# Cross-attention and FFN on one core: weighted sums in four column parts of 32, with their denominators in the second PSUM bank of the same tile

## The chip, the cores and the metric

The kernel runs on one core of a Trainium2 chip. Its engines work side by side, each in the order of its own queue: TensorE (PE, with its weight loads shown as PEld), VectorE (DVE), ScalarE (ACT), GpSimd (POOL) and SyncE (SP), which issues most transfers. The metric is the device time of one execution in microseconds (us), as the median of several runs.

## The reference

One sequence of 2048 rows of width 256 attends to 1601 context rows of width 192 plus one learned "null" key, with 16 heads of 64, and then passes through a three-layer network with weights of +1 and −1:

```python
x = layer_norm(_layernorm(x), g_norm)         # 2048 x 256
q = x @ Wq;  k, v = split(context @ Wkv)      # 16 heads of 64
k, v = [null_k; k], [null_v; v]               # 1602 keys
sim = einsum('bhid,bhjd->bhij', q * s, k * s) # s * s = 1/8
attn = softmax(where(mask, sim, -max))
out = einsum('bhij,bhjd->bhid', attn, v)
x = x0 + layer_norm(out @ Wout, g_out)
x = x + ffn(_layernorm(x))                    # 512 -> 1024 -> 1024 -> 256, relu * 2
```

All inputs but the masks are float32.

## The kernel before

The attention works in 32 units. A unit is a pair of heads (p, 8 of them) by a block of 512 query rows (b, 4 of them); in the code `u` counts the units. Keys are taken in KC = 13 chunks of 128 (the last has 66). The scores stand transposed, keys on the partitions and queries along the free axis, so that the exponentials can be used as the moving operand of the weighted sums without another transpose.

From the second unit on, a unit runs as follows, and the order is written out by hand (`manual_schedule`), engine by engine:

1. For each key chunk k: the scores of both heads (TensorE, L391; the first two chunks add the negated maximum of each query, L415), then the exponential on ScalarE (L417, `e`). Between them TensorE computes one chunk of row maxima for the *next* unit (L361, L345) into a PSUM tile, and VectorE reduces it (L364, L348). GpSimd adds up the exponentials of all chunks into `acc` (L665, L667), one sum for each key partition.
2. VectorE combines the maxima of the next unit (L369).
3. The denominators of the *previous* unit. In 28 units ("quarters": all but units 0, 1, 30 and 31) `denominators` (L443) multiplies `acc` by a matrix of ones: four matmuls of 32 columns and 256 queries, two for each head, which lie side by side in one PSUM bank, on 128 partitions by 256 columns. VectorE then takes the reciprocal (L455), ScalarE spreads it over the head's rows with eight small copies (L461), and VectorE multiplies the previous unit's weighted sums by it (L462, `aoT`). Units 1, 30 and 31 do it in `divided` after the third weighted chunk instead (L468, L470); the last unit's own division comes later, within the network.
4. The weighted sums of this unit (`weighted`, L424): for each of the 13 chunks, two matmuls of 64 columns, one a head. Head 0 goes to partitions 0 to 63 and head 1 to partitions 64 to 127 of one bank of `av`. Each float32 matmul appears in the trace as two records, one for each of two passes.
5. ScalarE copies the sums out (L721). TensorE turns the maxima of the next unit (L374), multiplies the previous unit's `aoT` by the output weights (L432), projects queries (L213) and a part of the next pair's keys (L243, L248) or values (L303, L315).

PSUM is divided between two pools of two tiles each, each tile two banks wide ([128, 2, 512] float32): `flex` (maxima, denominators, the turned maxima, projections) and `spare` (the two score tiles, `av`, the output projection). In `spare` the order within a unit is sT_1, sT_0, av, po, so that `av` takes over the buffer of the odd chunks' scores. A tile that is asked for waits until the tile two places back in its pool has been read. The waits between engines are semaphores that the framework sets from what each instruction reads and writes.

After the attention come the residual and the network, in blocks of 512 rows as well.

## Time and profile before

Three runs took 1289.89, 1290.35 and 1291.47 us; the median is 1290.35. One execution was profiled:

| what | value |
|---|---|
| span of the profiled execution | 1288.7 us |
| TensorE busy | 1275.8 us (99%) |
| GpSimd busy | 1001.7 us (78%) |
| VectorE busy | 787.9 us (61%) |
| ScalarE busy | 717.7 us (56%) |
| granted TensorE clock, mean | 1.000 |
| scores (L391), TensorE | 448.5 us |
| weighted sums (L424), TensorE | 364.7 us |
| maxima (L361), TensorE | 276.8 us |
| denominators (L443), TensorE | 17.9 us |
| reciprocals of the denominators (L455), VectorE | 48.9 us |

Busy time is the time in which at least one instruction of the group was under way. Matmuls overlap, so that the sum of their durations is larger than the busy time, and a busy TensorE is not one at its peak. In a timeline a row gives the start in us, the duration, the engine, the line, the operation and the tiles (out<-in), the number of instructions that were merged, and in brackets the engine's idle time ahead and what ended it.

### The profile page before, as it was taken

The page shows a single profiled execution, that of the slowest core. Times are in us where ns is not written, and L with a number is a line of the kernel's source. Part 1 is how long each engine was busy: PE and PEld are TensorE (multiplying, and loading weights), DVE is VectorE, ACT ScalarE, POOL GpSimd, SP SyncE. Part 2 cuts the span into 40 slices and gives each one's busy share as a digit, 9 for nine tenths or more (in the row PEclk, how much of TensorE's full clock was granted, in tenths as well). Part 3 has the DMA queues.
Part 4 walks back from the last instruction along what each step waited for, and adds up shares of the span by engine and source line. Part 5 has one row for each costly group of instructions (what it writes and reads, how often), then busy time and mean ns, then how long its engine had stood idle before and what let it go on. Part 6 is the DMA issues. An engine that isn't in the chain of part 4 may idle for free.

```text
span 1288.7 us, 16385 instructions
## 1 busy us (share of the span) xinstructions
PE 1275.8 (99%) x6672; PEld 648.9 (50%) x6672; DVE 787.9 (61%) x817; ACT 717.7 (56%) x965; POOL 1001.7 (78%) x508
## 2 busy tenths in 40 slices
PE   8999999999999999999999999999999999999998
PEld 6334444444444444444444444444444443788887
DVE  7887866655665566556666666666666784644432
ACT  4766556655555555555565666666655667422120
POOL 5798988998889888989899889988998999801100
PEclk9999999999999999999999999999999999999999
DMA  5000000000000000000000000000000010000000
GB/s 145 22 1 5 1 1 13 5 1 1 13 5 2 1 13 5 1 1 13 5 1 1 1 14 5 1 1 5 1 17 1 1 41 1 1 9 9 17 17 17
DMA packets 16156, 13.19 MB, mean 10 GB/s; under 512 B 2688, under 2 KB 15552, under 8 KB 16080
## 3 DMA queue, kind: packets, MB, share of 16 engines
q1 hardware_dynamic: 14944, 11.02, 3.1%
q8 instruction: 52, 0.85, 0.3%
q10 hardware_dynamic: 656, 0.79, 0.2%
q0 software_dynamic: 480, 0.34, 0.2%
q14 instruction: 24, 0.20, 0.1%
HBM read 10.04 MB, written 2.10 MB: 9 GB/s over the span
## 4 chain that ended last, share of the span: by engine, by line
PE 96%; DVE 2%; DMA 1%; ACT 1%; issue 0%; SPq 0%; DVEq 0%; ACTq 0%
PE sT L391 29%; PE av L424 27%; PE ps L775 11%; PE max L361 7%; PE po L432 4%; PE psq L213 4%; PE ps L806 2%; PE psv L303 2%; PE psk L243 1%; PE sT L415 1%; PE den L443 1%; PE psv L315 1%; DMA x_sb<-in_x 1%; PE psk L248 1%; PE max L345 1%; ACT e L417 1%
## 5 line engine op out<-in xcount | busy, mean ns | idle before, releaser
L667 POOL TENSOR_TENSOR acc<-acc,e 128x1024 f32<-128x1024 f32 (+1 forms) x352 | 847.3, 2407 | 27.6
L364 DVE TENSOR_REDUCE mx<-max 128x2 f32<-128x1024 f32 x384 | 450.3, 1220 | 80.3 <-PE max L361 78.4
L417 ACT ACTIVATE e<-sT,maskb 128x1024 f32<-128x1024 f32 (+1 forms) x416 | 460.4, 1113 | 40.4 <-PE sT L391 9.1
L391 PE MATMUL sT<-qT,kT 64*128 64x512 f32 (+1 forms) x1664 | 448.5, 613 | 1.5 <-ACT e L417 0.9
L424 PE MATMUL av<-e,v 128*64 128x512 f32 (+1 forms) x1664 | 364.7, 594 | 0.2 <-ACT e L417 0.2
L361 PE MATMUL max<-kr,qr 64*128 64x512 f32 x768 | 276.8, 712 | 1.9 <-DVE mx L364 1.9
L424 PEld LDWEIGHTS av<-e,v 128*64 128x64 f32 (+1 forms) x1664 | 116.7, 137 | 233.5 <-issue 230.5
L391 PEld LDWEIGHTS sT<-qT,kT 64*128 64x128 f32 (+1 forms) x1664 | 128.2, 181 | 146.6 <-ACT e L417 133.3
L461 ACT COPY aoT<-r 32x256 f32<-32x256 f32 x224 | 90.1, 402 | 63.9 <-DVE r L455 61.6
L361 PEld LDWEIGHTS max<-kr,qr 64*128 64x128 f32 x768 | 75.3, 187 | 95.8 <-DVE mx L364 67.4
L665 POOL TENSOR_TENSOR acc<-e,e 128x1024 f32<-128x1024 f32 x32 | 75.6, 2361 | 61.4 <-ACT seen L655 52.2
L721 ACT COPY avs<-av 128x512 f32<-128x512 f32 x32 | 18.7, 585 | 159.7 <-PE av L424 159.7
L462 DVE TENSOR_TENSOR aoT<-avs,aoT 128x512 f32<-128x512 f32 x28 | 43.1, 1539 | 94.3 <-ACT aoT L461 94.3
L376 DVE TENSOR_TENSOR mT<-mt,pick 128x512 fp32r<-128x512 f32 x32 | 22.1, 689 | 106.9 <-PE mt L374 106.9
L775 PE MATMUL ps<-h0hi,w 128*128 128x512 f32 x256 | 79.5, 392 | 0.0
L775 PE MATMUL ps<-h0lo,w 128*128 128x512 f32 x256 | 78.9, 389 | 0.0
L122 POOL TENSOR_TENSOR y_sb<-y_sb,gout_sb 128x256 f32<-128x256 f32 x12 | 9.3, 775 | 86.7 <-DVE y_sb L89 86.7
L214 ACT ACTIVATE qr<-psq 128x512 fp32r<-128x512 f32 x32 | 19.1, 597 | 97.8 <-PE psq L213 95.1
L763 ACT ACTIVATE h1hi<-ps 128x1024 fp32r<-128x1024 f32 x16 | 16.4, 1026 | 98.9 <-PE ps L775 98.9
L764 DVE SCALAR_TENSOR_TENSOR h1lo<-ps,h1hi 128x1024 fp32r<-128x1024 f32 x16 | 19.6, 1223 | 67.8 <-ACT h1hi L763 67.8
L432 PE MATMUL po<-wo,aoT 128*128 128x256 f32 x256 | 60.6, 379 | 0.0
L213 PE MATMUL psq<-xnT,wq 128*128 128x512 f32 x124 | 58.4, 593 | 0.6 <-ACT xnT L498 0.6
(164 smaller groups left out, 1135.4 us busy)
## 6 DMA issues: line engine op xcount, KB each, us to landing
out_x<-o SPq DMA_DIRECT2D x7, 256.0 KB, 2.2
x_sb<-in_x SPq DMA_DIRECT2D x3, 512.0 KB, 8.2
wa<-in_wkv SPq DMA_DIRECT2D x8, 128.0 KB, 2.7
wq<-in_wq SPq DMA_DIRECT2D x8, 128.0 KB, 2.2
wo<-in_wout SPq DMA_DIRECT2D x8, 128.0 KB, 2.0
xnT<-in_k SPq DMA_DIRECT2D x1, 1024.0 KB, 5.7
wb<-in_wkv SPq DMA_DIRECT2D x15, 64.0 KB, 2.4
ctx_a<-in_ctxT SPq DMA_DIRECT2D x2, 256.0 KB, 8.1
```

The lines of the kernel that those rows point to most:

```text
L213: nc.tensor.matmul(ps[:, 0, :], weights[p][0][:, c, :], xnT[:, b, c, :], start=c == 0, stop=c == 1)
L361: nc.tensor.matmul(ps[:, j, :w], qr[rows, ts(t, 128)], kr[rows, ds(start, w)], start=True, stop=True)
L364: nc.vector.tensor_reduce(maxima[p, b][:, t, :, c], ps[:, :, :w], AX.X, ALU.max)
L391: nc.tensor.matmul(ps[:n, j, :], kT[rows, ds(128 * k, n)], qT[rows, :], start=k < 2, stop=k >= 2, skip_group_check=k >= 2,)
L417: nc.scalar.activation(e[:n], ps[:n], AF.Exp, bias=maskb[:n, k : k + 1])
L424: nc.tensor.matmul(av[ts(j, DH), 0, :], v[:n, k, ts(j, DH)], e[:n, j, :], start=k == 0, stop=k == KC - 1)
L432: nc.tensor.matmul(pv[:, t, :], aoT[:, ts(t, 128)], weights[p][3], start=True, stop=True)
L461: nc.scalar.copy(aoT[ds(64 * j + 32 * rows, 32), ts(h, 256)], r[ds(64 * j + 32 * h, 32), :])
L462: nc.vector.tensor_tensor(aoT, avs, aoT, ALU.mult)
L665: nc.gpsimd.tensor_tensor(acc, es[0], es[1], ALU.add)
L667: nc.gpsimd.tensor_tensor(acc[:m], acc[:m], es[k][:m], ALU.add)
L775: nc.tensor.matmul(ps[:, f, :], w(c)[:, ts(2 * g + f, 128)], parts[part][:, c, :], start=i == 0, stop=i == len(steps) - 1,)
```

## The change

The weighted sums of a chunk are issued as four matmuls of 32 columns in place of two of 64: each head is divided in halves of its width, and the four parts go to partitions 0, 32, 64 and 96 on, each at its own column position of the array. Both halves of a head stream the same exponentials `e[:n, i // 2, :]`.

The `av` tile is asked for before the denominators, and in the 28 "quarters" units the denominators go to the first 256 columns of its second bank, which was idle. The weighted sums still go to its first bank. The flex tile for denominators is gone in these units; units 1, 30 and 31 keep theirs. The lines below L424 move down by five.

```diff
         def weighted(p, k, e, av):
             v = pairs[p][1]
             n = rows_of(k)
-            for j in range(2):
+            for i in range(4):
                 nc.tensor.matmul(
-                    av[ts(j, DH), 0, :], v[:n, k, ts(j, DH)], e[:n, j, :], start=k == 0, stop=k == KC - 1
+                    av[ts(i, 32), 0, :],
+                    v[:n, k, ts(i, 32)],
+                    e[:n, i // 2, :],
+                    start=k == 0,
+                    stop=k == KC - 1,
+                    tile_position=(0, 32 * i),
                 )
...
                 quarters = last is not None and u not in (1, len(units) - 2, len(units) - 1)
+                av = spare(f"av_{p}_{b}")
                 if quarters:
-                    den = flex(f"den_{p}_{b}")[:, 0, :256]
+                    den = av[:, 1, :256]
                     denominators(last[3], den)
                     aoT = divided_quarters(*last[:3], den)
-                av = spare(f"av_{p}_{b}")
                 for k in range(KC):
                     weighted(p, k, es[k], av)
```

## The prediction

> **What bounds the kernel now.** I read the page first (busy shares, the chain that ended last), then the timeline around one denominator, then the waits of TensorE and VectorE there, then the order and the waits of the built programs. The page:

> ```profile
> span 1288.7 us, 16385 instructions
> PE 1275.8 (99%) x6672; PEld 648.9 (50%) x6672; DVE 787.9 (61%) x817; ACT 717.7 (56%) x965; POOL 1001.7 (78%) x508
> ...
> PE 96%; DVE 2%; DMA 1%; ACT 1%; issue 0%; SPq 0%; DVEq 0%; ACTq 0%
> ...
> L424 PE MATMUL av<-e,v 128*64 128x512 f32 (+1 forms) x1664 | 364.7, 594 | 0.2 <-ACT e L417 0.2
> ```

> TensorE (PE) is on the chain for 96% of the span: whatever stops its queue is paid in full, and time that another engine gains is worth nothing. The weighted sums (L424) are 27% of that chain.

> The stretch that the change edits lies between the scores and the weighted sums of a unit. There is one such stretch in each of 28 units. The timeline, one of them (start, duration, engine, line):

> ```profile
> 388.33 7.23 POOL L667 TENSOR_TENSOR acc<-acc,e 128x1024 f32<-128x1024 f32 x3
> 389.65 0.80 PE L361 MATMUL max<-kr,qr 64*128 64x512 f32 x2
> 390.33 1.11 ACT L417 ACTIVATE e<-sT,maskb 66x1024 f32<-66x1024 f32 x1 [0.20 <-PE sT L391]
> 390.38 0.16 PEld L443 LDWEIGHTS den<-acc,ones 128*32 128x32 f32 x8 [0.56 <-issue]
> 390.38 0.64 PE L443 MATMUL den<-acc,ones 128*32 128x256 f32 x8
> 390.50 1.23 DVE L364 TENSOR_REDUCE mx<-max 128x2 f32<-128x1024 f32 x1 [0.41 <-PE max L361]
> 390.95 0.20 PEld L424 LDWEIGHTS av<-e,v 128*64 128x64 f32 x4 [0.41 <-issue]
> 390.95 4.08 PE L424 MATMUL av<-e,v 128*64 128x512 f32 x18
> 391.43 0.14 PEld L424 LDWEIGHTS av<-e,v 128*64 128x64 f32 x2 [0.29 <-issue]
> 391.75 0.19 DVE L369 TENSOR_REDUCE mcol<-mx 128x8 f32<-128x32 f32 x1
> 391.86 1.75 DVE L455 RECIPROCAL r<-den 128x256 f32<-128x256 f32 x1
> 391.86 0.14 PEld L424 LDWEIGHTS av<-e,v 128*64 128x64 f32 x2 [0.29 <-issue]
> 392.29 0.14 PEld L424 LDWEIGHTS av<-e,v 128*64 128x64 f32 x2 [0.29 <-issue]
> ...
> 393.64 1.23 ACT L461 COPY aoT<-r 32x256 f32<-32x256 f32 x3 [2.20 <-DVE r L455]
> ```

> Two things are to be seen. TensorE goes from the denominators (390.38) to the weighted sums (390.95) at once. And VectorE is far behind it: it still has the last maximum (1.23), the combined maximum (0.19) and only then the reciprocal of the denominators, which ends at 391.86 + 1.75 = 393.61. Today nobody on TensorE waits for that: the reciprocal's reader is ScalarE, and its result is wanted only at the output projection after the weighted sums (402.4).

> **The change, part by part.**

> *The denominators in the second bank of av (28 units).* This removes a flex tile and adds a wait. In the built program of before, the first weighted matmul waits only for ScalarE's exponentials (L417). In that of the changed kernel, in all 28 units, it waits for VectorE's count to reach the reciprocal of the denominators in the same tile: the tile is guarded as if the two banks were one. The weighted sums overwrite no column that the reciprocal reads, but the semaphore holds them all the same. Behind that matmul in the in-order TensorE queue are all weighted sums, the transposed maxima (L374), the output projection, the next queries and keys or values, and so the next unit's scores; ACT, DVE and POOL wait for those.

> Price: the first weighted load starts at 390.95 and could start when the reciprocal is done, 393.61: 2.66 us here, 2.65 to 2.66 in all 28 units (mean 2.653). Add the step from VectorE's end to TensorE's start, which the profile shows where TensorE does wait for VectorE:

> ```profile
> 36.53 0.69 DVE L376 TENSOR_TENSOR mT<-mt,pick 128x512 fp32r<-128x512 f32 x1 [0.92 <-PE mt L374]
> 37.28 0.19 PEld L415 LDWEIGHTS sT<-mT,ones_r 64*128 64x128 f32 x2 [0.62 <-DVE mT L376]
> ```

> 37.28 − 37.22 = 0.06. So 2.71 a unit, 28 × 2.71 = 75.9 us, none of it beside other TensorE work, as nothing may overtake in that queue. The reciprocal can't come sooner: the maximum ahead of it waits for the last max matmul (390.45), and the denominators end (391.02) before VectorE is free, so their start doesn't matter.

> [...]

> *What the freed flex tile gives.* The denominators waited for the maximum two chunks back (L348), now for the exponential of k = 11; both are over by 390.3. The flex tiles that follow (mt, queries, keys or values, first maxima) are still two tiles behind an engine that is done, so no wait goes: 0. Spare tiles go round in the same order as before. The orders of ACT, DVE, POOL and SP are unchanged, and no DMA moves.

> *Four parts of 32 columns.* 104 instead of 52 weighted matmul records a unit, and as many weight loads. With two parts of 64 the loads come in pairs every 0.43 us (391.43, 391.86, 392.29): both heads stream side by side, and a key chunk costs two such slots. Each part still streams 512 columns of e in two passes, so if four run side by side the slot stays 0.43. The nearest row is the denominators themselves, four parts of 32 with 256 columns: 8 records in 0.64, the second four starting 0.24 after the first, against 0.43 / 2 = 0.215 for the same columns. So four do run side by side. That 0.24 is a first slot; the weighted sums' own first slot is 0.48 for a steady 0.43, an excess of 0.05 against 0.025. I take 0.43, that is 0 us. Upper end: the 0.025 in each of the 25 further slots, 25 × 32 units × 0.025 = +20 us. Lower end: the shorter first slot, 32 × 0.025 = −0.8 us; more can't go, since the streamed columns stay.

> *Units 1, 30 and 31* keep their denominators (L468) in a flex tile after chunk 2, and have no new wait. There 64-column denominators now stand between 32-column sums. Going from the denominators' 32 columns to the sums' 64 costs about 0.11 today (second four at 390.62, plus 0.215, to 390.95); twice in three units that is at most 0.7 us, and cancels the −0.8.

> *The clock.* TensorE is granted 1.00 throughout; its longest idle stretch once warm is 1.54 us, and the clock held through it:

> ```profile
> 74.47 0.50 PE L361 MATMUL max<-kr,qr 64*128 64x512 f32 x2 [1.54 <-DVE mx L364]
> ```

> The new gaps are 2.65 us (391.02 to 393.67), longer than any shown. I take no loss.

> [...]

> **Sum.** 1288.7 + 75.9 + 0 = 1364.6 of span; the median of the three runs lies 1.65 above the profiled span (1290.35), so 1366.2.

> **The rivals.**
> 1. *Four parts stream more slowly than two.* For it: 104 loads and 104 matmuls a unit must be issued in 11.3 us, and 0.24 against 0.215 above. Against: L315 issues 16 matmuls and 16 loads inside 1.16 us. Up to +20: 1386.
> 2. *Parts run only two at a time* (steady slots four a chunk): 13 × 2 × 0.43 × 32 = +358, 1724. Against it: the denominators' 0.64 us for 8 records; two at a time would need four slots, 0.86.
> 3. *The gaps cost clock.* Nothing in the profile shows a gap of this length, so the price is bounded from the rows by 0 and by the whole of the following weighted sums at half speed, 28 × 11.3 = +316; an intermediate loss of a tenth of that gives about 1400.
> 4. *The change does what it says, no slower than before.* The 75.9 us would have to come back from the sums. This decides where a slot falls from 0.43 to 0.43 − 75.9 / (26 × 32) = 0.34 us. Against: 0.24 for 256 columns in four parts is no faster a column than 0.43 for 512 in two. Then 1290 or less.
> 5. *The wait is over sooner than read:* only if VectorE did the reciprocal ahead of the maximum (the wait then ends with the denominators + 1.75, about 392.8, 1.9 us a unit, 1343). Its order is unchanged, so I give it little.

> **How the numbers follow.** Forecast (wait as priced, slot within 0.003 of 0.43: 1364 to 1369): 0.78. Rival 1: 0.10. Rival 2: 0.02. Rival 3: 0.06. Rival 4: 0.02. Rival 5: 0.02. The range leaves out rivals 2, 4, 5 and most of 3: 1358 to 1392. Slower by over 0.2% (2.6 us, about what a measurement of this kernel can tell) in all but rival 4: 0.98; faster 0.01, same 0.01.

> **What the changed profile would show.** Right: 28 waits at the weighted sums' line, released by VectorE's reciprocal, of about 3.1 us on the weight loads (390.54 to 393.67) and 2.65 on the matmuls (74 us in total); VectorE's share of the chain that ended last up from 2% to about 8% (390.45 to 393.61 in each unit), 3.6% of it the reciprocal; the weighted sums of a unit still 11.3 us, with twice the records; clock 1.00. Wrong: weighted sums longer than 11.4 us a unit (rivals 1, 2), a clock under 1.00 (3), or no wait at that line (4, 5).

## The result and the profile after

The changed kernel took 1398.51 us (median of 4 runs, 1397.45 to 1399.88) against 1290.38 us before (median of 4): a ratio of 1.0839, 95% interval 1.0827 to 1.0852, 108 us slower. The prediction was 1366.2 us, in a range of 1358 to 1392. The direction and the wait were right, and 32 us were missing. The profiled execution has a span of 1397.7 us, 109.0 more than before.

The page after, with the lines that answer to those shown before:

```profile
span 1397.7 us, 19706 instructions
PE 1311.4 (94%) x8336; PEld 644.1 (46%) x8336; DVE 788.0 (56%) x817; ACT 717.5 (51%) x965; POOL 1003.3 (72%) x508
...
PE 91%; DVE 7%; DMA 1%; ACT 1%; issue 0%; SPq 0%; DVEq 0%; ACTq 0%
...
L424 PE MATMUL av<-e,v 128*32 128x512 f32 (+1 forms) x3328 | 396.4, 636 | 74.0 <-DVE r L460 73.8
```

VectorE is now on the chain that ended last for 7% of the span, where it was 2%. The weighted sums stand still for 74 us behind the reciprocal (the last column; 0.2 us before). But they are also 32 us busier, 396.4 us for 364.7: that second sum has nothing to do with waiting.

The waits (who waited for what: us in total, times, longest) give the size of one stop:

```profile
PEld av L424 <- DVE r L460: 87.3, 28, 3.1
...
PE av L424 <- DVE r L460: 73.8, 28, 2.6
```

There are 28 stops of 2.64 us for the matmuls and 3.12 us for the weight loads; the prediction had 2.65 and 3.1.

The timeline of two units (start, duration):

```profile
421.45 0.64 PE L448 MATMUL av<-acc,ones 128*32 128x256 f32 x8
421.56 1.23 DVE L364 TENSOR_REDUCE mx<-max 128x2 f32<-128x1024 f32 x1 [0.41 <-PE max L361]
422.82 0.19 DVE L369 TENSOR_REDUCE mcol<-mx 128x8 f32<-128x32 f32 x1
422.92 1.75 DVE L460 RECIPROCAL r<-av 128x256 f32<-128x256 f32 x1
...
424.72 13.02 PE L424 MATMUL av<-e,v 128*32 128x512 f32 x104 [2.64 <-DVE r L460]
459.88 0.64 PE L448 MATMUL av<-acc,ones 128*32 128x256 f32 x8
463.16 11.37 PE L424 MATMUL av<-e,v 128*32 128x512 f32 x104 [2.64 <-DVE r L460]
```

From the denominators to the sums it is now 424.72 − 421.45 = 3.27 us, for 0.57 before: 2.70 more, as priced. What was not foreseen is the duration of the sums: the same 104 records take 13.02 us in one unit and 11.37 in the next. The granted clock explains it. The view of whole stretches (start:end, length, busy time and count of PE, PEld, DVE, ACT, POOL, then the granted TensorE clock, and last the DMA share and its GB/s) around the first unit's sums, and of the second unit's:

```profile
421.20:424.61 3.41, 0.89 (x12) 0.16 (x8) 3.02 (x3) 1.11 (x1) 3.25 (x3) 1.00 0.00 0
424.61:428.02 3.41, 3.30 (x16) 0.80 (x20) 0.06 (x1) 3.22 (x8) 3.33 (x2) 0.51 0.00 0
428.02:431.43 3.41, 3.41 (x36) 0.96 (x32) 1.56 (x1) 0.00 (x0) 3.33 (x2) 0.99 0.00 0
459.60:463.10 3.50, 0.92 (x12) 0.16 (x8) 3.07 (x3) 1.14 (x2) 3.34 (x3) 1.00 0.00 0
463.16:466.57 3.41, 3.41 (x32) 1.07 (x36) 0.10 (x1) 3.20 (x8) 3.33 (x2) 1.00 0.00 0
```

After the first gap the clock is granted at about half for one stretch of 3.41 us (16 matmul records fall into it where 32 or 36 do at full clock), after the second it is not. Over the whole execution:

```profile
core 0: 1397.7 us, clock 0.976
```

(1 − 0.976) × 1397.7 = 33.5 us lost. The trace's record of the clock has 20 stretches of 3.41 us at half before the last matmul: 20 × 1.7 = 34. Of these 19 follow one of the 28 gaps (19 × 1.7 = 32.4; theory A below speaks of 20). The other stands at 21.9 us, in the start-up, ahead of the first gap at 123.6 (0.50 from 21.92 to 25.33 us, where the profile before has 1.00). The profiled run of the parts alone, which has none of the gaps, is not at 1.000 either (0.999). The whole difference: 28 × 2.70 = 75.6 for the wait, 32.4 for the clock after the gaps, and 1.5 from the start-up (the first weighted sums begin at 53.63 us, at 52.14 before) make 109.5, for a measured 109.0.

### The profile page after: what moved, and what is told of

Its sections match the earlier page's. It is cut to its first block, busy times and chain, and to the rows that moved or that the text cites. A ratio compares the mean times of both kernels' runs of the same rounds, so it can differ in the third digit from the quotient of the medians.

```text
span 1397.7 us, 19706 instructions
## 1 busy us (share of the span) xinstructions
PE 1311.4 (94%) x8336; PEld 644.1 (46%) x8336; DVE 788.0 (56%) x817; ACT 717.5 (51%) x965; POOL 1003.3 (72%) x508
## 4 chain that ended last, share of the span: by engine, by line
PE 91%; DVE 7%; DMA 1%; ACT 1%; issue 0%; SPq 0%; DVEq 0%; ACTq 0%
PE av L424 28%; PE sT L391 27%; PE ps L780 10%; PE max L361 6%; PE po L437 4%; PE psq L213 4%; DVE r L460 3%; DVE mx L364 3%; PE ps L811 2%; PE psv L303 1%; PE psk L243 1%; PE sT L415 1%; PE psv L315 1%; DMA x_sb<-in_x 1%; PE psk L248 1%; PE max L345 1%
## 5 line engine op out<-in xcount | busy, mean ns | idle before, releaser
L364 DVE TENSOR_REDUCE mx<-max 128x2 f32<-128x1024 f32 x384 | 450.3, 1220 | 82.4 <-PE max L361 80.6
L417 ACT ACTIVATE e<-sT,maskb 128x1024 f32<-128x1024 f32 (+1 forms) x416 | 460.3, 1113 | 40.6 <-PE sT L391 8.5
L424 PE MATMUL av<-e,v 128*32 128x512 f32 (+1 forms) x3328 | 396.4, 636 | 74.0 <-DVE r L460 73.8
L391 PE MATMUL sT<-qT,kT 64*128 64x512 f32 (+1 forms) x1664 | 448.8, 613 | 1.4 <-ACT e L417 0.9
L361 PE MATMUL max<-kr,qr 64*128 64x512 f32 x768 | 277.8, 713 | 2.3 <-DVE mx L364 2.3
L424 PEld LDWEIGHTS av<-e,v 128*32 128x32 f32 (+1 forms) x3328 | 110.0, 116 | 347.1 <-issue 257.1
L391 PEld LDWEIGHTS sT<-qT,kT 64*128 64x128 f32 (+1 forms) x1664 | 128.6, 181 | 146.1 <-ACT e L417 132.8
L376 DVE TENSOR_TENSOR mT<-mt,pick 128x512 fp32r<-128x512 f32 x32 | 22.1, 691 | 211.7 <-PE mt L374 211.7
L670 POOL TENSOR_TENSOR acc<-e,e 128x1024 f32<-128x1024 f32 x32 | 75.6, 2363 | 89.7 <-ACT seen L660 80.2
L361 PEld LDWEIGHTS max<-kr,qr 64*128 64x128 f32 x768 | 75.8, 187 | 96.1 <-DVE mx L364 68.0
L266 POOL TENSOR_TENSOR kT<-kT 128x256 f32<-128x256 f32 (+1 forms) x48 | 31.8, 663 | 46.7 <-DVE kr L255 43.5
```

What stands on the lines that cost most here:

```text
L361: nc.tensor.matmul(ps[:, j, :w], qr[rows, ts(t, 128)], kr[rows, ds(start, w)], start=True, stop=True)
L364: nc.vector.tensor_reduce(maxima[p, b][:, t, :, c], ps[:, :, :w], AX.X, ALU.max)
L391: nc.tensor.matmul(ps[:n, j, :], kT[rows, ds(128 * k, n)], qT[rows, :], start=k < 2, stop=k >= 2, skip_group_check=k >= 2,)
L417: nc.scalar.activation(e[:n], ps[:n], AF.Exp, bias=maskb[:n, k : k + 1])
L424: nc.tensor.matmul(av[ts(i, 32), 0, :], v[:n, k, ts(i, 32)], e[:n, i // 2, :], start=k == 0, stop=k == KC - 1, tile_position=(0, 32 * i),)
L670: nc.gpsimd.tensor_tensor(acc, es[0], es[1], ALU.add)
```

## The experiments

Theory A: the guard on the shared tile makes 28 gaps, and the clock answers most of them. Its rivals: the four parts themselves cost the missing 32 us (B), the clock has no part in them (C), or any gap can set the clock off (D).

**The four parts alone.** The denominators stay in their flex tile, ahead of `av`.

```diff
-                av = spare(f"av_{p}_{b}")
                 if quarters:
-                    den = av[:, 1, :256]
+                    den = flex(f"den_{p}_{b}")[:, 0, :256]
                     denominators(last[3], den)
                     aoT = divided_quarters(*last[:3], den)
+                av = spare(f"av_{p}_{b}")
```

> The weighted sums in four parts of 32, with the denominators left in their flex tile. Theory A (the guard on the shared tile costs 28 gaps of 2.64 us = 74 us, and the 20 stretches at half clock that follow gaps cost 20 x 1.7 = 34 us; the parts cost nothing): no wait for the reciprocal, clock 1.00, slots of 0.43 us; denominators and sums now share one array shape, so the 0.11 us between them goes in 28 units: 1290.4 - 3 = about 1287. Theory B (the four parts themselves cost the 32 us that the prediction missed, for instance by drawing the clock down): about 1322.

Measured: 1286.89 us (11 runs) against 1289.70 (15 runs), ratio 0.9976, interval 0.9967 to 0.9985. Theory A's number, and B is out: the parts cost nothing and make the kernel a little faster than before. The timeline:

```profile
391.05 0.64 PE L448 MATMUL den<-acc,ones 128*32 128x256 f32 x8
...
391.51 11.34 PE L424 MATMUL av<-e,v 128*32 128x512 f32 x104
...
392.53 1.75 DVE L460 RECIPROCAL r<-den 128x256 f32<-128x256 f32 x1
```

The sums start 0.46 us after the denominators for 0.57 before (28 × 0.11 = 3.1 us), and take 11.34 for 11.38. The reciprocal starts 1.02 us after the sums, and no matmul waits for it. This is the fastest of all kernels here.

**The second bank alone.** The weighted sums go back to two parts of 64.

```diff
-            for i in range(4):
+            for j in range(2):
                 nc.tensor.matmul(
-                    av[ts(i, 32), 0, :], v[:n, k, ts(i, 32)], e[:n, i // 2, :], ..., tile_position=(0, 32 * i),
+                    av[ts(j, DH), 0, :], v[:n, k, ts(j, DH)], e[:n, j, :], ...
```

> The denominators in the second bank of av, the weighted sums still in two parts of 64. Theory A: the same 28 gaps of about 2.64 us and about as many stretches at half clock as after the whole change (20, give or take 5, as the gaps fall on the clock's grid): 1390 to 1407. Theory B: the wait alone, clock 1.00: about 1366.

Measured: 1397.85 us against 1289.70, ratio 1.0838 (1.0823 to 1.0852). The whole loss, without the parts. Waits and clock are those of the whole change: (1 − 0.977) × 1395.3 = 32 us of clock lost, for 33.5 there:

```profile
PEld av L424 <- DVE r L455: 87.3, 28, 3.1
PE av L424 <- DVE r L455: 73.8, 28, 2.6
```

```profile
core 0: 1395.3 us, clock 0.977
```

**TensorE kept at work through the wait.** The whole change, with matmuls that nobody reads:

```diff
                     den = av[:, 1, :256]
                     denominators(last[3], den)
+                    fill = flex(f"fill_{p}_{b}")
+                    for _ in range(3):
+                        nc.tensor.matmul(fill[:, 0, :512], ident, es[0][:, 0, :512], start=True, stop=True)
```

> The whole change, and three matmuls of 512 columns that nobody reads (ident by e, 0.86 us each, into a flex tile) between denominators and weighted sums, so that TensorE works through the wait. Theory A: the wait stays, the clock stays at 1.00, and only the 28 x 2.71 remain: about 1366. Theory C (the 32 us are not the clock's answer to an idle TensorE but a cost of the wait or of the four parts): about 1398 as after the change.

Measured: 1367.32 us against 1289.70, ratio 1.0601 (1.0586 to 1.0615). Its timeline:

```profile
413.13 0.64 PE L448 MATMUL av<-acc,ones 128*32 128x256 f32 x8
413.70 2.84 PE L703 MATMUL fill<-e,ident 128*128 128x512 f32 x6
414.60 1.75 DVE L460 RECIPROCAL r<-av 128x256 f32<-128x256 f32 x1
...
416.47 1.06 PE L424 MATMUL av<-e,v 128*32 128x512 f32 x8
```

The sums still start only when the reciprocal is over (3.34 us after the denominators), and yet the kernel is 31 us faster than the changed one, for doing more work. The clock is held:

```profile
core 0: 1366.9 us, clock 0.999
```

So the wait itself is worth 1367 − 1290 = 77 us, and the clock's answer to the idle TensorE the other 31. C is out.

**One such matmul in place of three** (`range(1)`).

> The whole change, and one such matmul of 0.86 us in the gap, which leaves about 1.75 us idle. After the change the clock halved where 2.4 us or more of one 3.41 us stretch of its grid were idle, and did not where 1.94 us or less were. Theory A with that threshold: no stretch at half clock, 1366. Theory D (it is a matter of the gap's place and any gap longer than the 1.5 us of before can do it): some stretches at half clock, 1375 to 1398.

Measured: 1366.79 us, ratio 1.0595 (1.0576 to 1.0615), clock 0.999. Gaps of 1.58 us remain, 28 of them (44.3 us in total), and the clock loses (1 − 0.999) × 1366.1 = 1.4 us in the whole execution, for 33.5 after the change:

```profile
PE av L424 <- DVE r L460: 44.3, 28, 1.6
```

```profile
core 0: 1366.1 us, clock 0.999
```

D is out, at least for gaps of 1.6 us.

**The reciprocal ahead of the last maximum.** The denominators and the division are issued before the last max chunk of the unit, so that on VectorE the reciprocal no longer stands behind the last maximum:

```diff
                     es.append(exps(p, b, k, sT))
+                    if k == KC - 1:
+                        av = spare(f"av_{p}_{b}")
+                        if quarters:
+                            den = av[:, 1, :256]
+                            denominators(last[3], den)
+                            aoT = divided_quarters(*last[:3], den)
                     if nxt is not None:
                         max_chunk(*nxt, order[k])
...
-                av = spare(f"av_{p}_{b}")
-                if quarters:
-                    den = av[:, 1, :256]
-                    denominators(last[3], den)
-                    aoT = divided_quarters(*last[:3], den)
```

> The whole change, with the denominators and the division issued ahead of the last max chunk, so that on VectorE the reciprocal comes before the last maximum (1.23) and the combined maximum (0.19). Theory A: the price of the wait is what VectorE has to do ahead of the reciprocal's end; the sums now start about 1.75 us later than without the wait in place of 2.71, the gap is about 1.5 us and no stretch has half clock: 1290 + 28 x 1.75 = about 1339. If the wait's price were a fixed cost of the shared tile, independent of VectorE's order: 1366 to 1398.

Measured: 1340.44 us against 1289.47, ratio 1.0394 (1.0364 to 1.0424). The timeline:

```profile
403.73 0.64 PE L448 MATMUL av<-acc,ones 128*32 128x256 f32 x8
404.30 0.50 PE L361 MATMUL max<-kr,qr 64*128 64x512 f32 x2
404.42 1.76 DVE L460 RECIPROCAL r<-av 128x256 f32<-128x256 f32 x1 [0.89 <-PE av L448]
...
406.24 1.06 PE L424 MATMUL av<-e,v 128*32 128x512 f32 x8 [1.44 <-DVE r L460]
```

VectorE now waits for the denominators, and the sums for 1.44 us only. So the price of the guard follows from what VectorE has to do up to the reciprocal's end: 51 us here, 77 with the last maximum and the combined maximum ahead of it.

**Shorter fillers, for idle times between 1.6 and 2.6 us.** As the filler above, one matmul of 256 and one of 128 columns.

> The whole change and one unread matmul of 256 columns (0.43 us) in the gap, which leaves about 2.0 us idle. Theory A, if the clock's bound lies above 2.0 us of a 3.41 us stretch: no half clock, 1366. If it lies between 1.94 and 2.0: some stretches at half clock, 1375 or more.

> The whole change and one unread matmul of 128 columns (0.21 us), which leaves about 2.2 us idle, between the 1.94 that did not halve the clock and the 2.43 that did. No half clock (1366) puts the bound above 2.2; 15 or more stretches at half clock (1390 to 1400) put it below.

Measured, one run each: 1399.18 and 1400.77 us against 1289.47, clocks of 0.976 and 0.974. The timeline and the clock after one gap of the first:

```profile
421.63 0.70 PE L703 MATMUL fill<-e,ident 128*128 128x256 f32 x2
424.34 4.05 PE L424 MATMUL av<-e,v 128*32 128x512 f32 x20 [2.01 <-DVE r L460]
```

```profile
424.20:427.60 3.40, 3.26 (x20) 0.99 (x24) 0.08 (x1) 3.20 (x8) 3.32 (x2) 0.58 0.00 0
```

The gaps are 2.01 us in the first and about 2.2 in the second (the estimate written down), and the clock loses no less than with those of 2.64: (1 − 0.976) × 1397.3 = 33.5 and (1 − 0.974) × 1399.0 = 36.4 us, for 33.5. For both, the first of the two answers written down (no half clock) was wrong and the second right: gaps of 2.01 us were enough.

**The reciprocal twice** (a second identical `nc.vector.reciprocal(r, ps)`), which lengthens the gap by 1.75 us.

> The whole change with VectorE's reciprocal of the denominators done twice, which lengthens the wait by 28 x 1.75 = 49 us to gaps of 4.39 us. Theory A: nearly every gap now leaves 2.4 us or more of one stretch of the clock's grid idle, so 24 to 28 stretches at half clock, some of them partly over before the sums start: 1366 + 49 + 30 to 48 = 1445 to 1463. If the clock's part did not depend on the length of the gap: 1398 + 49 = 1447 with 20 stretches.

Measured, one run: 1484.87 us against 1289.47, above the expected range.

```profile
403.77 0.64 PE L448 MATMUL av<-acc,ones 128*32 128x256 f32 x8
408.84 14.17 PE L424 MATMUL av<-e,v 128*32 128x512 f32 x104 [4.43 <-DVE r L461]
```

```profile
PEld av L424 <- DVE r L461: 137.5, 28, 4.9
PE av L424 <- DVE r L461: 124.0, 28, 4.4
```

```profile
core 0: 1483.1 us, clock 0.942
```

The wait did as expected: (124.0 − 73.8) = 50 us more than after the change. The clock lost more than theory A said: (1 − 0.942) × 1483.1 = 86 us, what 50 stretches of 3.41 us at half clock would cost (an estimate, at 1.7 each), for the 24 to 28 written down. The sums of the unit shown take 14.17 us, 2.80 more than at full clock after the change (11.37), where one such stretch made them 1.65 longer there (13.02). The sums start 408.84 − 403.77 = 5.07 us after the denominators, for 0.57 before; with 28 × 4.50 = 126 for this wait, 69 of the 195 measured remain for the clock. That is 17 less than the 86 of its record: an estimate is that these 17 fell into the wait itself, where TensorE had no work to slow down.

## Why the prediction was wrong

- *What bounds the kernel, and the wait on the reciprocal*: right. 28 gaps, 2.64 us each on the matmuls; with the clock held, the kernel takes 1366.8 and 1367.3 us, for a forecast of 1366.2.
- *The four parts stream as two did*: right. The slot is 0.43 us, the sums of a unit 11.37 at full clock.
- *The clock, "I take no loss"*: this is the step that failed. The longest idle stretch in the profile before was 1.54 us and the new gaps were 2.65, so the profile had no row for them; I took the value at the near end and let a chance of 0.06 stand for everything beyond. The runs showed a half-clock stretch after 19 of the 28 gaps, 32 us of the 109, and its absence once TensorE had work in the gaps (clock 0.999, 1367.32 and 1366.79 us). The rival on the clock was the case that came true, and the range left it out. That its "about 1400" lies so near 1398.5 is luck: it was a tenth of a bound, and no row stood behind the tenth. Nor did a row of before that the prediction shows have the half speed of that bound: the run after the change showed it, 0.51 in the stretch from 424.61 us, but for 3.41 us after 19 of the gaps and not for the whole of the sums after 28. With a filler that left 2.01 us idle in each gap the clock was 0.976 too.
- *The 0.11 us between denominators and sums*: the prediction priced it for units 1, 30 and 31 only. In the 28 others the wait hides that it goes. With the denominators back in their own tile the kernel gains 2.8 us (0.24%). In units 1, 30 and 31 the stretch from the first sum to the next other work, with the denominators between, takes 12.45 us for 12.17: 0.8 us in all, for a priced 0.7 at most.
- Whether the chip needs the guard between two banks of one tile stays open: taking the wait alone away was not tried.

## What to carry to other kernels

Here the framework made a write to one bank of a tile wait for a read of the other bank. Putting a small result into an idle half of a tile that TensorE is about to fill ties the two together, and the price is set by all that the reader's engine still has to do up to the end of the read (77 us here, 51 with the reciprocal ahead of the two maxima). And a wait on this TensorE-bound kernel had two prices: its length, and, after 19 of the 28 gaps of 2.64 us, a stretch of 3.41 us at half clock (32 us in all), which matmuls that nobody reads kept off (clock 0.999 for 0.976). Where a profile has no row as long as a new gap, the clock's answer belongs in the range with weight.
